# Layer 0's softmax sums from ones beside the values, moved into place by DMA

## The chip, the cores and the metric

The kernel runs on one core of one Trainium2 chip. The metric is device time in microseconds for one execution of the whole program. Several executions are timed and the median is given; one further execution is recorded by the hardware profiler, and all durations of single instructions come from that one.

## The reference

Four layers work on a batch of 16 sequences of 100 tokens with width 256 (`x`) and a context of 16 x 361 x 256 (`ctx_1024`). Only layer 0 matters for the change. It is a transformer decoder layer with 16 heads of 16 columns: masked self-attention, then cross-attention to the context, then a feed-forward layer, each followed by a layer norm.

```python
def _mha(xq, xk, xv, ..., causal):
    q, k, v = projections of xq, xk, xv              # (batch, 16 heads, tokens, 16)
    s = jnp.einsum('bhqe,bhke->bhqk', q, k) * (1.0 / math.sqrt(256))
    if causal: s = jnp.where(mask, s, -jnp.inf)
    w = jax.nn.softmax(s, axis=-1)                   # exp(s - max) / sum of exp
    o = jnp.einsum('bhqk,bhke->bhqe', w, v)
    return o (heads side by side) @ Wo.T + bo
```

The change concerns the division by the sum of the exponentials. Layer 1 (4 heads of 64), layer 2 (8 heads of 32 and a recurrent scan) and layer 3 follow and are not changed in what they do.

## The kernel before, in words

Activations are kept transposed, with the width on 128 partitions in two chunks (`c`), and in four groups (`g`) of four batches each, 400 columns a group. Products that need full precision are split into a high and a low part and made as three matmuls (`mm3`, L293). The order of the work on TensorE (PE), VectorE (DVE), ScalarE (ACT) and GpSimd (POOL) is the order in which the Python code issues it. Only the order of the DMA queue on SyncE (SP) is set by a scheduler, by its own estimate of times. Work that may run between the steps of a phase is written as generators and kept in a `Flow`: `flow.fill()` lets every generator in its side list take one step (the lists of weights, and `recips`) and then lets others run until one of them has issued matmuls. A generator that yields `REST` lets a step pass.

**Self-attention of layer 0** (`self_phase` with `nh` = 16) loops over 16 batches with two units each. A unit makes scores for eight heads in two PSUM banks (L1135, onto a mask, L854), takes maxima on DVE (L866), exponentials on ACT (L268), transposes on PE (L886) and copies those to SBUF on ACT (L595). When both units of a batch are done, `weigh` multiplies the transposed exponentials with the values (L588). The values of a batch lie in a tile `va` in which each head has 32 columns (`wide`): an even head has its 16 values in the first 16 of them, an odd head in the last 16, and the other 16 columns are zero. So the results of an even and an odd head, added in PSUM, land on the two halves of the same 32 partitions. The same pairs are formed once more with `cnt16` in place of the values (L903), 16 columns of ones and 16 of zeros: this gives each head's sum on the very partitions where its output is. ACT copies sums (L910) and outputs (L912), DVE takes the reciprocal (L913), POOL multiplies (L914), and `split_o` writes the high and low parts of the product to `oP` (POOL, L560 and L561). After every fourth batch the output projection follows (`epi_s0`).

Beside this phase, `split_context` brings the context in (L760), splits it on POOL (cast L763, difference L764) and stores both parts to DRAM (L496), one batch's part a step. Loads of it come back at L769, weights at L354.

**Cross-attention of layer 0** (`cross_phase` with `nh` = 16) loops over 16 batches with four units of four heads. The plan `"S01AV2Bb3CDmam"` gives the order within a unit: S scores (L824), digits maxima (L643), A to D the exponentials (L268, which also accumulate the sum of each row), a and b transposes (L665) with copies (L595 on ACT, L597 on DVE), V the weighing of the unit before the last (L588), m an attempt to finish a batch, followed by `flow.fill()`. DVE adds the odd heads' unit to the even heads' (L682, L684). The row sums of a batch's 16 heads go through `recips`: a reciprocal on DVE (L543), an expansion to 256 columns on ACT (L546), two transposes on PE (L553) and a copy on ACT (L555); POOL multiplies (L700). After the loop, `tail` issues what is left of the last two units among the first steps of the feed-forward phase.

Of the kernel before, what the change touches and what calls it, by code (L numbers as in the profile page):

```python
# [13 lines left out]
ALU = mybir.AluOpType  # L14
# [33 lines left out]
def tile_chain(ctx: ExitStack, tc: tile.TileContext, a: dict, out: bass.AP):  # L48
# [67 lines left out]
    nc.vector.tensor_reduce(parity[:, 0:1], sel4, AX.X, ALU.add)  # L116
    nc.vector.tensor_scalar(parity[:, 1:2], parity[:, 0:1], -1.0, 1.0, ALU.mult, ALU.add)

    cnt = const.tile([S, 112], F32, name="cnt")
    nc.gpsimd.memset(cnt, 1.0)  # L120
    nc.gpsimd.memset(cnt[:, 16:32], 0.0)
    cnt16 = [cnt[:, 0:32], cnt[:, 16:48]]
    cnt64 = cnt[:, 48:112]

    pexp = [const.tile([S, 4 * S], F32, name=f"P{i}") for i in range(6)]

    vals = []
    for i in range(2):
        t = const.tile([TC, NTC, 512], F32, name=f"va{i}")
        nc.gpsimd.memset(t, 0.0)  # L130
        vals.append(t)
    vals4 = [t[:, :, i * D : (i + 1) * D] for t in vals for i in range(2)]
    turns = {}
# [403 lines left out]
    def recips(ps, sums, nh, rests):  # L537
# [17 lines left out]
        nc.scalar.copy(rT, tp[:, : 2 * S])  # L555
        return rT

    def split_o(of, oP, bl):
        sl = slice(bl * S, (bl + 1) * S)
        nc.gpsimd.tensor_copy(oP[:, 0, :, sl], of)  # L560
        nc.gpsimd.tensor_tensor(oP[:, 1, :, sl], of, oP[:, 0, :, sl], ALU.subtract)  # L561
# [37 lines left out]
    def cross_phase(ps, nh, pro, load_kv, score, epi, plan, after=None, started=False, beat=None, late=None, **sets):  # L599

        units = head_units(nh)
        nu = nh // 4
        seq = [(b, u) for b in range(NB) for u in range(nu)]
        N = len(seq)
        kv, q, of, pts, pTs, total, scs, nms = {}, {}, {}, {}, {}, {}, {}, {}  # L610
        done, ended = [-1], []

        def kv_of(b):

            flow.front(
                ("kv", b), load_kv(b, lambda: nh != 16 or done[0] >= b - 2 and all(o[0] != "t" for o, _ in flow.q))
            )

        if not started:
            flow.put(("q", 0), pro(0))  # L620
            kv_of(0)

        def scores(n):
            b, u = seq[n]
            g, bl = b // GB, b % GB
            if u == 0:
                if bl == 0:
                    q[g] = flow.need(("q", g))
                    q[g, "o"] = pair(name="oP")
                    if g + 1 < NG:  # L630
                        flow.put(("q", g + 1), pro(g + 1))
                    elif after is not None:
                        after()
                kv[b] = flow.need(("kv", b))
                if b + 1 < NB:
                    kv_of(b + 1)
                total[b] = small.tile([S, 16], F32, tag="sums", name="sums")
            scs[n] = [ps.tile([P, 512], F32, tag="sc", name="sc") for _ in range(4)]
            score(q[g], bl, kv[b][0], units[u], scs[n])

        def high(n, i):
            nms[n, i] = nm = small.tile([S, 1], F32, tag="nm1", name="nm1", bufs=6)
            nc.vector.tensor_reduce(nm, scs[n][i][:S, :T], AX.X, ALU.max, negate=True)  # L643

        def soft(n, i):
            b, u = seq[n]
            h = units[u][i]
            pts[n, i] = pt = turn("P", pexp)
            look_up(
                pt[:, :T], scs[n][i][:S, :T], AF.Exp, **sets, bias=nms.pop((n, i)), accum_out=total[b][:, h : h + 1]  # L650
            )
            if i == 3:
                scs.pop(n)
                if u == nu - 1:
                    flow.put(("r", b), recips(ps, total.pop(b), nh, plan[plan.index("D") :].count("m")))

        def turned(n, *heads, tag="tp"):

            tps = []
            for i, _ in heads:  # L660
                pt = pts.pop((n, i))
                tp = ps.tile([P, 512], F32, tag=tag, name="pT_ps")
                made[0] += 1
                for c in range(NTC):
                    nc.tensor.transpose(tp[:TC, c * S : (c + 1) * S], pt[:, c * TC : (c + 1) * TC], ident[:S, :S])  # L665
                tps.append(tp)
            for (i, act), tp in zip(heads, tps):
                pTs[n, i] = pT = att.tile([P, 4 * S], F32, tag="pT", name="pT", bufs=NPT)
                evac(pT[:TC, : NTC * S], tp[:TC, : NTC * S], act)

        def weigh(n):
            b, u = seq[n]
            g, bl = b // GB, b % GB
            if u == 0:
                of[b] = att.tile([P, 2, S], F32, tag="of", name="of")
            o = ps.tile([P, 512], F32, tag="o", name="o_ps")
            made[0] += 1
            values(o, units[u], nh, kv[b][1], TC, lambda k, i: pTs[n, i][:TC, k * S : (k + 1) * S], NTC, nh > 4)
            if nh == 4:
                nc.vector.tensor_copy(of[b], o[:, : 2 * S].rearrange("p (c s) -> p c s", c=2))  # L680
            elif nh == 16 and u % 2:
                nc.vector.tensor_tensor(of[b][:, u // 2], o[:, :S], of[b][:, u // 2], ALU.add)  # L682
            else:
                nc.vector.tensor_copy(of[b][:, u // 2 if nh == 16 else u], o[:, :S])  # L684
            for i in range(4):
                pTs.pop((n, i))
            if u == nu - 1:
                kv.pop(b)
                done[0] = b
                ended.append(b)  # L690

        def finish():

            if not ended:
                return
            b = ended.pop()
            g, bl = b // GB, b % GB
            rT = flow.need(("r", b))
            f = of.pop(b)
            nc.gpsimd.tensor_tensor(f, f, rT.rearrange("p (c s) -> p c s", c=2), ALU.mult)  # L700
            split_o(f, q[g, "o"], bl)
            if bl == GB - 1:
                flow.put(("e", g), epi(g, q[g, "o"]))

        for n in range(N):
            for what in plan:
                if what == "S":
                    scores(n)
                    if n == 0 and flow.tailed():

                        flow.fill(2)
                    if n == 0:
                        clear_pads()
                elif what in "0123":
                    high(n, "0123".index(what))
                elif what in "ABCD":
                    soft(n, "ABCD".index(what))
                elif what == "a":
                    turned(n, (0, False), (1, True))
                elif what in "pq":  # L720
                    turned(n, ("pq".index(what), what == "q"))
                elif what == "V" and n >= 2:
                    weigh(n - 2)
                elif what == "V" and n == 0:
                    flow.end("t")
                elif what == "b" and n >= 1:
                    turned(n - 1, (2, False), (3, nh != 16))
                elif what in "rt" and n >= 1:
                    turned(n - 1, (2 + "rt".index(what), what == "t"))
                elif what == "m":  # L730
                    finish()
                    flow.fill()
                elif what == "s":
                    beat()

        def tail():

            weigh(N - 2)
            yield
            finish()  # L740
            turned(N - 1, (2, False), tag="mm")
            yield
            turned(N - 1, (3, True), tag="mm")
            yield
            weigh(N - 1)
            finish()
            yield

        if late is not None:
            late()  # L750
        flow.front(("t", None), tail())
# [76 lines left out]
    def self_phase(ps, nh, pro, w, score, epi, mask=None, beside=None, after=None, started=False):  # L828
# [61 lines left out]
                piece[b, h] = pT[:S, i * S : (i + 1) * S]  # L890

        def weigh(b):
            g, bl = b // GB, b % GB
            o = ps.tile([P, 512], F32, tag="o", name="o_ps")
            units = head_units(nh)
            half = len(units) // 2 or 1
            for us in (units[:half], units[half:]):
                for hs in us:
                    values(o, hs, nh, va[b], S, lambda k, i: piece[b, hs[i]], 1)
                for hs in us:  # L900
                    for h in hs:
                        c, r, cols, new, end = place(h, nh)
                        nc.tensor.matmul(  # L903
                            o[r, (2 + c) * S : (3 + c) * S], lhsT=cnt16[h % 2] if nh == 16 else cnt64,
                            rhs=piece.pop((b, h)), start=new, stop=end,
                        )
            va.pop(b)
            made[0] += 1
# [2 lines left out]
            of = att.tile([P, 2, S], F32, tag="of", name="of")  # L911
            nc.scalar.copy(of, o[:, : 2 * S].rearrange("p (c s) -> p c s", c=2))  # L912
            nc.vector.reciprocal(r, r)  # L913
            nc.gpsimd.tensor_tensor(of, of, r, ALU.mult)  # L914
            split_o(of, q[g, "o"], bl)
            if bl == GB - 1:
                flow.put(("e", g), epi(g, q[g, "o"]))

        def self_v(b):
            X, bl = q[b // GB][0], b % GB  # L920
# [787 lines left out]
```

## Time and profile before

| what | us |
|---|---|
| three timed executions | 1618.21, 1619.55 and 1625.3; median 1619.55 |
| the profiled execution, its own time | 1609.87 |
| its span from first to last instruction | 1608.2 |
| self-attention of layer 0, about | 25 to 205 |
| cross-attention of layer 0, about | 200 to 530 |
| granted TensorE clock, mean over the span | 0.959 of full |
| count matmuls with 32 columns (L903), whole span | 512 records, 21.7 busy |
| transposes of the expanded reciprocals (L553), all layers | 96 records, 16.8 busy |
| transfers issued on SP, whole span | 175 |

How to read it: the profile of one execution lists busy time of each engine, groups of equal instructions (count, busy time, mean length of one, idle time of the engine in front of them and what ended it), and the chain of waits: followed back from the last instruction, at each step to what released it. "PEld" is the weight load of TensorE and overlaps its matmuls. An fp32 matmul can appear as two records. "Granted clock" is the share of TensorE's full clock that the chip allowed in a stretch. SP has no busy time; its rows are the issues of transfers.

### The profile page before, as it was taken

The page shows a single profiled execution, that of the slowest core. Times are in us where ns is not written, and L with a number is a line of the kernel's source. Part 1 is how long each engine was busy: PE and PEld are TensorE (multiplying, and loading weights), DVE is VectorE, ACT ScalarE, POOL GpSimd, SP SyncE. Part 2 cuts the span into 40 slices and gives each one's busy share as a digit, 9 for nine tenths or more (in the row PEclk, how much of TensorE's full clock was granted, in tenths as well). Part 3 has the DMA queues.
Part 4 walks back from the last instruction along what each step waited for, and adds up shares of the span by engine and source line. Part 5 has one row for each costly group of instructions (what it writes and reads, how often), then busy time and mean ns, then how long its engine had stood idle before and what let it go on. Part 6 is the DMA issues. An engine that isn't in the chain of part 4 may idle for free.

```text
span 1608.2 us, 34891 instructions
## 1 busy us (share of the span) xinstructions
PE 1496.7 (93%) x13528; PEld 1320.5 (82%) x13528; DVE 924.6 (57%) x2137; ACT 811.4 (50%) x2301; POOL 692.6 (43%) x1136
## 2 busy tenths in 40 slices
PE   8999989999999989889999999998999999989998
PEld 6777777877777878779998889997888888878987
DVE  4565667777777663655534345556555555655553
ACT  4656756766766344641135553215455555555333
POOL 3435635565332445842257663133144444553300
PEclk9897999999998998999999999999999999998999
DMA  3343331121111000100013330010011111112085
GB/s 113 109 129 113 118 99 46 52 59 52 39 40 38 20 27 14 35 14 14 14 42 99 95 116 23 25 40 20 20 39 45 51 39 39 52 39 85 1 230 174
DMA packets 76501, 97.30 MB, mean 61 GB/s; under 512 B 3840, under 2 KB 76336, under 8 KB 76336
## 3 DMA queue, kind: packets, MB, share of 16 engines
q1 hardware_dynamic: 76336, 95.07, 19.7%
q8 instruction: 107, 1.75, 0.4%
q14 instruction: 58, 0.48, 0.1%
HBM read 81.49 MB, written 13.57 MB: 59 GB/s over the span
## 4 chain that ended last, share of the span: by engine, by line
PE 61%; DVE 11%; POOL 8%; ACT 8%; issue 8%; DMA 2%; SPq 0%; ACTq 0%; POOLq 0%; DVEq 0%
PE up_ps L293 12%; PE pT_ps L665 7%; PE down_ps L293 7%; PE lin_ps L293 5%; PE v_ps L293 5%; PE o_ps L588 5%; PE k_ps L293 4%; PE sc L824 4%; PE h_ps L1442 4%; ACT P L268 3%; DVE nm L643 2%; DMA cx<-cx 2%; PE pT_ps L886 2%; ACT L263 1%; PE sc L1135 1%
## 5 line engine op out<-in xcount | busy, mean ns | idle before, releaser
L268 ACT ACTIVATE P<-sc,nm 100x361 f32<-100x361 f32 (+1 forms) x678 | 314.2, 497 | 184.3 <-DVE nm L643 144.2
L643 DVE TENSOR_REDUCE nm<-sc 100x1 f32<-100x361 f32 x448 | 222.8, 525 | 100.5 <-PE sc L824 98.2
L665 PE MATMUL pT_ps<-ident,P 100*121 100x100 f32 x1344 | 212.8, 287 | 25.7 <-DVE pT L597 12.4
L293 PE MATMUL up_ps<-xp,w 128*128 128x400 f32 x1152 | 234.6, 354 | 2.2 <-DVE xp L300 1.1
L665 PEld LDWEIGHTS pT_ps<-ident,P 100*121 100x121 f32 x1344 | 176.4, 190 | 62.7 <-ACT P L268 20.8
L293 PEld LDWEIGHTS up_ps<-xp,w 128*128 128x128 f32 x1152 | 213.9, 192 | 7.9 <-DVE xp L300 2.0
L304 POOL TENSOR_TENSOR hp<-hid,hp 128x400 fp32r<-128x400 f32 x64 | 69.9, 1093 | 232.5 <-DVE hp L300 206.1
L293 PE MATMUL down_ps<-hp,w 128*128 128x400 f32 x768 | 155.8, 350 | 4.9 <-DVE x L988 1.8
L293 PEld LDWEIGHTS down_ps<-hp,w 128*128 128x128 f32 x768 | 141.3, 190 | 9.3 <-POOL hp L304 3.6
L597 DVE COPY pT<-pT_ps 121x300 f32<-121x300 f32 x287 | 127.1, 460 | 31.8 <-PE pT_ps L665 30.5
L588 PE MATMUL o_ps<-pT,va 121*32 121x100 f32 (+3 forms) x3328 | 127.6, 262 | 14.7 <-ACT f L322 2.8
L595 ACT COPY pT<-pT_ps 121x300 f32<-121x300 f32 (+2 forms) x273 | 110.9, 421 | 59.4 <-PE pT_ps L886 38.6
L588 PEld LDWEIGHTS o_ps<-pT,va 121*32 121x32 f32 (+3 forms) x3328 | 90.1, 118 | 56.6 <-issue 15.1
L293 PE MATMUL v_ps<-w,cx 128*121 128x256 f32 x864 | 131.5, 294 | 0.1
L293 PE MATMUL k_ps<-cx,w 128*128 128x362 f32 x576 | 116.8, 342 | 5.9 <-DMA cx<-cx 4.0
L293 PE MATMUL lin_ps<-xp,w 128*128 128x400 f32 x480 | 112.6, 375 | 8.0 <-DVE xp L300 5.2
L293 PEld LDWEIGHTS v_ps<-w,cx 128*121 128x121 f32 x864 | 110.6, 185 | 2.0 <-DVE of L682 0.5
L268 ACT ACTIVATE hid<-up_ps 128x400 f32<-128x400 f32 x64 | 32.4, 506 | 157.6 <-PE up_ps L293 148.9
L1442 PE MATMUL h_ps<-ht,raw 128*128 128x96 f32 (+4 forms) x792 | 107.8, 279 | 3.3 <-POOL ht L1456 1.6
L1442 PEld LDWEIGHTS h_ps<-ht,raw 128*128 128x128 f32 x792 | 98.1, 193 | 8.3 <-POOL ht L1456 7.1
L293 PEld LDWEIGHTS lin_ps<-xp,w 128*128 128x128 f32 x480 | 90.5, 203 | 14.3 <-DVE xp L300 4.9
L293 PEld LDWEIGHTS k_ps<-cx,w 128*128 128x128 f32 x576 | 94.6, 191 | 7.8 <-issue 4.4
(198 smaller groups left out, 2599.6 us busy)
## 6 DMA issues: line engine op xcount, KB each, us to landing
cx<-cx SPq DMA_DIRECT2D x80, 728.0 KB, 5.7
raw<-in_ctxT SPq DMA_DIRECT2D x16, 364.0 KB, 5.3
ct<-in_ctxp SPq DMA_DIRECT2D x16, 363.0 KB
raw<-in_L_Wf SPq DMA_DIRECT2D x8, 256.0 KB, 2.8
x<-in_xT SPq DMA_DIRECT2D x4, 400.0 KB
out<-y SPq DMA_DIRECT2D x8, 200.0 KB
raw<-in_L_ff_W1T SPq DMA_DIRECT2D x4, 256.0 KB
raw<-in_L_ff_W2T SPq DMA_DIRECT2D x4, 256.0 KB, 2.6
```

Source lines behind the costliest of these rows:

```text
L263: load = nc.scalar.preload_act_table_set(SETS[table["set"]][0]).ins
L268: table["used"].append(nc.scalar.activation(out_, in_, func, **kw).ins)
L293: nc.tensor.matmul(dst, lhsT=l, rhs=r, start=first and i == 0, stop=last and i == n - 1)
L304: nc.gpsimd.tensor_tensor(lo, src, hi, ALU.subtract)
L588: nc.tensor.matmul(o[r, at : at + S], lhsT=va[:rows, k, cols], rhs=pT(k, i), start=(new or alone) and k == 0, stop=(end or alone) and k == ...
L595: nc.scalar.copy(dst, src)
L597: nc.vector.tensor_copy(dst, src)
L643: nc.vector.tensor_reduce(nm, scs[n][i][:S, :T], AX.X, ALU.max, negate=True)
L665: nc.tensor.transpose(tp[:TC, c * S : (c + 1) * S], pt[:, c * TC : (c + 1) * TC], ident[:S, :S])
L824: nc.tensor.matmul(sc[:S, :TE], lhsT=lhs, rhs=k[r, lk, c, :TE], start=n == 0, stop=n == 2)
L886: nc.tensor.transpose(tp[:S, i * S : (i + 1) * S], pt[:, i * S : (i + 1) * S], ident[:S, :S])
L1442: nc.tensor.matmul(v[:, c], lhsT=wgh[:, k, c * P : (c + 1) * P], rhs=ht[:, k, :, t - n : t], start=k == 0, stop=k == 1,)
```

## The change

`va` is filled with ones instead of zeros (the values of each batch overwrite only their own 16 of 32 columns). A matmul with 32 columns of `va` then gives a head's output on 16 partitions and the head's sum on the 16 beside them. Even and odd heads are no longer added in PSUM but kept apart: `s4` has room for both (`[P, 2, 2, S]`, the first 2 for even and odd). `unmix` moves the 16-partition pieces with DMAs on SP: for each of even and odd and each of four 32-partition blocks, one transfer brings the sums onto the partitions of the outputs (`r`) and one brings the outputs (`of`). That is 16 transfers of 16 partitions x 200 elements a batch, for 16 batches of self-attention and 16 of cross-attention. `inverse` takes 1/r on ACT as Exp(-Ln r), after three (self) or four (cross) steps of its generator. In cross-attention the exponentials no longer accumulate sums, `recips` is not used for `nh` = 16, `finish` passes by as long as the inverse is not issued, and `tail` forces it. The sums and the count matmuls of self-attention (L903) are gone for `nh` = 16; layer 1 keeps them.

```diff
-    cnt = const.tile([S, 112], F32, name="cnt")
-    nc.gpsimd.memset(cnt, 1.0)
-    nc.gpsimd.memset(cnt[:, 16:32], 0.0)
-    cnt16 = [cnt[:, 0:32], cnt[:, 16:48]]
-    cnt64 = cnt[:, 48:112]
+    cnt64 = const.tile([S, 64], F32, name="cnt64")
+    nc.gpsimd.memset(cnt64, 1.0)
...
         t = const.tile([TC, NTC, 512], F32, name=f"va{i}")
-        nc.gpsimd.memset(t, 0.0)
+        nc.gpsimd.memset(t, 1.0)
...
+    def unmix(s4):
+        of = att.tile([P, 2, S], F32, tag="of", name="of")
+        r = att.tile([P, 2, S], F32, tag="rT", name="rT")
+        for i in range(2):
+            for j in range(P // 32):
+                own, other = (slice(32 * j + 16 * k, 32 * j + 16 * k + 16) for k in (i, 1 - i))
+                nc.sync.dma_start(r[own], s4[other, i])
+                nc.sync.dma_start(of[own], s4[own, i])
+        return of, r
+
+    def inverse(r, rests):
+        for _ in range(rests):
+            yield REST
+        look_up(r, r, AF.Ln)
+        look_up(r, r, AF.Exp, scale=-1.0)
+        return r
...
@@ cross_phase, soft @@
-            look_up(
-                pt[:, :T], scs[n][i][:S, :T], AF.Exp, **sets, bias=nms.pop((n, i)), accum_out=total[b][:, h : h + 1]
-            )
+            kw = {} if nh == 16 else {"accum_out": total[b][:, h : h + 1]}
+            look_up(pt[:, :T], scs[n][i][:S, :T], AF.Exp, **sets, bias=nms.pop((n, i)), **kw)
             if i == 3:
                 scs.pop(n)
-                if u == nu - 1:
+                if u == nu - 1 and nh != 16:
                     flow.put(("r", b), recips(ps, total.pop(b), nh, plan[plan.index("D") :].count("m")))
...
@@ cross_phase, weigh @@
-            if u == 0:
+            if u == 0 and nh == 16:
+                of[b] = twos[0].tile([P, 2, 2, S], F32, tag="s4", name="s4")
+            elif u == 0:
                 of[b] = att.tile([P, 2, S], F32, tag="of", name="of")
...
-            elif nh == 16 and u % 2:
-                nc.vector.tensor_tensor(of[b][:, u // 2], o[:, :S], of[b][:, u // 2], ALU.add)
             else:
-                nc.vector.tensor_copy(of[b][:, u // 2 if nh == 16 else u], o[:, :S])
+                nc.vector.tensor_copy(of[b][:, u % 2, u // 2] if nh == 16 else of[b][:, u], o[:, :S])
...
+                if nh == 16:
+                    of[b], r = unmix(of[b])
+                    flow.put(("r", b), inverse(r, 4))
 
-        def finish():
+        def finish(now=False):
 
-            if not ended:
+            if not ended or nh == 16 and not now and ("r", ended[-1]) not in flow.got:
                 return
...
@@ cross_phase, tail @@
+            finish(True)
             weigh(N - 2)
             yield
-            finish()
+            finish(True)
...
             weigh(N - 1)
-            finish()
+            if nh == 16:
+                yield REST
+                yield REST
+            finish(True)
             yield
...
@@ self_phase, weigh @@
+            if nh == 16:
+                made[0] += 1
+                for u, hs in enumerate(units):
+                    at = (u % 2 * 2 + u // 2) * S
+                    values(o[:, at : at + S], hs, nh, va[b], S, lambda k, i: piece.pop((b, hs[i])), 1, True)
+                va.pop(b)
+                s4 = twos[0].tile([P, 2, 2, S], F32, tag="s4", name="s4")
+                nc.scalar.copy(s4, o[:, : 4 * S].rearrange("p (i c s) -> p i c s", i=2, c=2))
+                of, r = unmix(s4)
+                flow.put(("w", ("out", b)), ending(b, of, r))
+                return
...
+        def outputs(b, of, r):
+            g, bl = b // GB, b % GB
             nc.gpsimd.tensor_tensor(of, of, r, ALU.mult)
             split_o(of, q[g, "o"], bl)
             if bl == GB - 1:
                 flow.put(("e", g), epi(g, q[g, "o"]))
+
+        def ending(b, of, r):
+            r = yield from inverse(r, 3)
+            outputs(b, of, r)
```

Lines in `@@` name the function that a piece is in.

## The prediction

> **What bounds the kernel now.** I read four views: the page, then busy time by stretch, then groups of instructions and the order of time in layer 0. From the page:
>
> ```profile
> PE 1496.7 (93%) x13528; PEld 1320.5 (82%) x13528; DVE 924.6 (57%) x2137; ACT 811.4 (50%) x2301; POOL 692.6 (43%) x1136
> PE 61%; DVE 11%; POOL 8%; ACT 8%; issue 8%; DMA 2%; SPq 0%; ACTq 0%; POOLq 0%; DVEq 0%
> ```
>
> TensorE is busy 93% of the span and holds 61% of the chain that ended last. Is that so where the change works? Busy time in two stretches, self-attention and cross-attention of layer 0 (columns: stretch, its length, then busy us and count of PE, PEld, DVE, ACT, POOL, then granted clock, DMA share, GB/s):
>
> ```profile
> 25.00:183.00 158.00, 146.90 (x1794) 118.13 (x1794) 93.03 (x166) 95.28 (x294) 67.65 (x80) 0.87 0.35 108
> 205.00:530.00 325.00, 300.76 (x3654) 245.41 (x3655) 234.22 (x590) 218.21 (x686) 145.76 (x180) 0.95 0.17 50
> ```
>
> PE is busy 93% of both, every other engine under 75%. So work taken off PE counts nearly in full, and the other engines matter where PE waits for them. Idle PE is 11 us in the first and 24 us in the second: a ceiling on what shorter waits can give.
>
> **Self-attention, removed.** The end of a batch's weighing, in order of time (start, length):
>
> ```profile
> 102.09 0.53 PE L903 MATMUL o_ps<-pT,cnt 100*32 100x100 f32 x16
> 102.43 0.53 PE L588 MATMUL o_ps<-pT,va 100*32 100x100 f32 x16
> 102.77 0.53 PE L903 MATMUL o_ps<-pT,cnt 100*32 100x100 f32 x16
> 103.42 0.33 ACT L910 COPY rT<-o_ps 128x200 f32<-128x200 f32 x1 [0.84 <-PE o_ps L903]
> 103.78 1.40 DVE L913 RECIPROCAL rT<-rT 128x200 f32<-128x200 f32 x1 [1.32 <-ACT rT L910]
> ```
>
> Blocks of 16 records start 0.34 us apart (102.09, 102.43, 102.77). The two counting blocks (L903) go, the value blocks stay: 2 x 0.34 x 16 batches = **-11 us**. The reciprocal leaves VectorE, 1.40 us and the wait in front of it (27.3 us in 13 times). VectorE has room; what PE gains lies between 0 and the 11 us that it idles. PE's named waits there are mostly for other work, so I take **-1**.
>
> **Self-attention, added.** ScalarE loses two copies (0.344 + 0.356 us), gains one of 128x400 (nearest row: 100x400, 0.50) and Ln and Exp of 128x200 (between a copy, 0.36, and the 128x400 Ln, 0.59; I take 0.40 each): +0.6 a batch, 10 us in all, hidden, since ScalarE is busy 95 of 158 us. Ln and Exp are in the table set already loaded.
>
> **The transfers.** Each of 32 batches gets 16 transfers on SP, each 16 partitions of 800 bytes. No row shows one of this shape. Nearest rows:
>
> ```profile
> 102.06 0.37 SPq L496 DMA_DIRECT2D cx<-cx  x1
> 65.43 0.37 SPq L496 DMA_DIRECT2D cx<-cx  x1
> 65.85 0.50 SPq L354 DMA_DIRECT2D raw<-in_L_c_WkT  x1
> L1315 SPq DMA_DIRECT2D raw<-in_L_Wg x1: 557/557/557, 1029.4 to 1029.4; - x1
> L1316 SPq DMA_DIRECT2D raw<-in_L_Wgc x1: 584/584/584, 1030.0 to 1030.0; - x1
> raw<-in_L_ff_W2T SPq DMA_DIRECT2D x4, 256.0 KB, 2.6
> cx<-cx SPq DMA_DIRECT2D x80, 728.0 KB, 5.7
> ```
>
> A lone issue is 0.37 us, back to back they start 0.42 to 0.51 apart, and transfers of 64 partitions take 0.56 and 0.58. I take 0.46, in the middle of the back-to-back rows, with ends 0.37 and 0.58. Landing: 2.6 us (256 KB row); below it only smaller, above it 5.7 if a cx transfer is ahead. So a batch's sums arrive 16 x 0.46 + 2.6 = 10.0 us after the copy that they read. In the program each transfer also waits for the one eight places before it: right behind a cx store of 5.7 us the eighth is held 5.7 - 8 x 0.46 = 2.0 us.
>
> The Trainium skill, page "DMA: Bandwidth & Descriptors", section "Rules for kernel authors", speaks against this: many small transfers should be coalesced, and under 64 KB one pays mostly overhead. The same page ("Anatomy of one DMA", fitted for transfers issued from GpSimd) gives about 2.0 us fixed; with that landing the 10.0 would be an estimated 9.4.
>
> Is 10.0 us too long in self-attention? Its period is (191.73 - 38.2) / 14 = 11.0 us (first copy L910 to the fifteenth), so about 10.3 afterwards. In ScalarE's order of the changed program Ln stands one batch plus two pT copies, a va copy and two heads' Exps behind the copy: 10.3 + about 3 = 13 us. Slack 3 us. SP's own load: 16 x 0.46, plus 34 older transfers in 14 batches, 2.4 x 0.46 = 1.1, makes 8.5 of 10.3 us. Behind a late Ln on ScalarE stand PE's pT copies; behind POOL's product stand the casts and differences of cx (0.92 + 1.75 us), and behind those, on SP, the store of cx and the next batch's transfers. That ring (0.75 Ln and Exp, 1.6 POOL, 2.7 cx, 0.9 two issues, 10.0) is 16 us against two periods, 20.6.
>
> **Cross-attention.** Removed on PE: two transposes a batch (L553, 0.26 us each if apart; overlapped pairs take 0.34 to 0.36): 0.26 to 0.36 x 16, I take **-5**. On ScalarE:
>
> ```profile
> L268 ACT ACTIVATION_READ_ACCUMULATOR P<-sc,nm 100x1 f32 x254 | 49.8, 196 | 0.0
> L546 ACT COPY rx<-rs 100x256 f32<-100x256 f32 x16 | 6.6, 413 | 1.4 <-DVE rs L543 1.4
> L555 ACT COPY rT<-rT_ps 128x200 f32<-128x200 f32 x16 | 5.1, 316 | 0.0
> ```
>
> The accumulator reads go. They overlap their neighbours: Exps start 0.55 us apart with them (330.45, 331.00, 331.54), 0.48 without (98.72, 99.20; wider data), so each costs 0.07 or a little more. rx and rT (0.73) make room for Ln and Exp (0.8). PE waits 19.9 us for these Exps in 26 places (pT_ps, L665); 0 to -6, I take **-2**.
>
> The added wait: the copy that ends a batch corresponds to the first row below, and Ln now stands behind the last Exp two units later:
>
> ```profile
> 335.45 0.25 DVE L682 TENSOR_TENSOR of<-o_ps,of 128x100 f32<-128x100 f32 x1
> 337.43 0.56 ACT L268 ACTIVATE P<-sc,nm 100x361 f32<-100x361 f32 x1 [0.50 <-DVE nm L643]
> 343.00 0.74 PE L824 MATMUL sc<-kc,two 32*100 32x362 f32 x12
> ```
>
> Unit starts are 333.78, 338.51, 343.00; the fourth Exp comes 3.65 after a start, so Ln stands at 343.00 + 3.65 + 0.5 = 347.1, which is 11.4 us behind the copy's end (335.7). Needed: 10.0. **Slack 1.4 us**, thin. Weight loads that wait for POOL stand within some batches' transfers on SP, cutting batches in halves. For late Lns in both phases: 0 to +8, I take **+1.5**.
>
> **The two ends.** From 190.65 to 208.5 the chain of waits runs through POOL's last cx, two stores and two loads of cx and into k_ps. Eight transfers of batch 15 now stand before the last store, eight behind: 0 to 16 x 0.46 = 7.4; I take **+3**. At the end of cross-attention the last copy ends at 530.1, so its sums land at 540.1, while Ln stands behind the fourth Gelu (534.7), with two table loads (1.28 each) and 0.8 around it. ScalarE is held 5.4 + 3.4 = 8.8 us; PE can run ahead on four score banks, about 5 us: 0 to +8.8, I take **+3.5**.
>
> **Sum**: -11 - 1 - 5 - 2 + 1.5 + 3 + 3.5 = **-11 us**. Against the profiled execution, 1609.87 (span 1608.2 and 1.7 around it): 1598.9. The median shown is 1619.55, 9.7 above; the same difference gives **1608.6** (-0.7%). About 0.5%, 8 us, is what a measurement here can tell from no change.
>
> **Rivals.** (1) **Sums come late in cross-attention**, the slower one: ScalarE stands at Ln and PE behind its Exps. It decides from (11.4 - 2.6) / 16 = 0.55 us a transfer, and in self-attention from (10.3 - 1.1) / 16 = 0.575. At 0.65, 16 x 0.10 = 1.6 us late in cross and 1.2 in self, over 16 batches each: +26 and +19, so -11 + 45 = +34, 1653. For it: the 64-partition rows. Against it: all full-width rows. At 0.58 it is only 0.5 us late in cross, 0.1 in self: -11 + 8 + 1, about -2.
> (2) **Gain eaten**: issue near 0.58, or transfers behind 5.7 us of cx in many batches, or the ends at their upper bounds (+10): -11 + 9 to 12, 1619.
> (3) **PE waits shrink too**: -12 - 4 - 6 - 6 + 3 = -25, 1594.
> That the change does nothing of what it says I can exclude: value copies write 16 of each 32 columns, so the ones stay, and the counting matmuls and transposes are gone from PE's order.
>
> **Numbers.** Forecast 0.42 (0.35 beyond 0.5%, 0.07 within), rival 3 0.10, rival 2 0.18 within, rival 1 0.30 slower. So faster 0.45, same 0.25, slower 0.30. The range runs from rival 3 (1594) into rival 1, to 1645; the faster cases alone span 1594 to 1611.
>
> **What would show it.** The stretch of self-attention shorter by 8 to 12 us and cross-attention by 3 to 7, no L903 form with 32 columns, issues near 0.46 on SP, and few waits of ScalarE for DMA at Ln. Wrong if ScalarE's waits for rT add up to tens of us, if SP is occupied without a gap in self-attention, or if the ends cost over 10 us.

## The result and the profile after

The changed kernel takes **1661.2 us**, the median of four executions (1655.95 to 1668.0), against 1620.3 for the kernel before, also of four (1618.21 to 1625.3). The ratio is **1.0258, with a 95% interval of 1.023 to 1.0286**: 41 us slower, where 11 us faster was forecast.

The profiled execution of the changed kernel is the slowest of its four (1668.0 us, span 1666.3), that of before (1609.87) is faster than all four of its own. So the two traces lie 58 us apart, 17 more than the medians; verdicts below go by the timed runs, the traces tell where. Three executions of the kernels below, one each of e4, e5 and e14 (1655.6, 5937.0 and 1631.6 us), were slow and are left out of the ratios, though not of the medians.

The page of after, in the two places that were shown of before:

```profile
PE 1505.9 (90%) x12984; PEld 1325.9 (80%) x12984; DVE 914.1 (55%) x2105; ACT 806.5 (48%) x2063; POOL 692.6 (42%) x1135
PE 54%; DVE 12%; issue 8%; POOL 8%; ACT 8%; SPq 5%; DMA 4%; ACTq 0%; DVEq 0%; POOLq 0%
```

TensorE has 544 records fewer and yet 9 us more of busy time. A queue that had 0% of the chain, SPq, now has 5%, and DMA has 4% for 2%.

Busy time by stretch (columns as before). First self-attention, then 40 us behind it, then cross-attention, moved by 44 us against the stretch shown of before:

```profile
25.00:183.00 158.00, 134.10 (x1207) 106.23 (x1208) 78.72 (x142) 90.77 (x275) 59.92 (x67) 0.78 0.32 96
225.00:245.00 20.00, 3.49 (x38) 2.70 (x38) 1.77 (x5) 3.58 (x9) 9.10 (x18) 0.61 0.44 138
245.00:265.00 20.00, 10.48 (x78) 8.32 (x77) 4.23 (x11) 5.03 (x11) 6.08 (x10) 0.53 0.36 114
249.00:574.00 325.00, 296.82 (x3629) 242.16 (x3630) 231.38 (x571) 201.57 (x430) 143.41 (x177) 0.95 0.20 58
```

Cross-attention is as it was (300.8 us of PE before, clock 0.95). Self-attention is not: all engines do less in the same 158 us, and the granted clock is 0.78 for 0.87. Behind it TensorE all but stands, 3.5 us of work in 20.

What SP does (order of time; start, length of the issue):

```profile
102.48 0.53 SPq L493 DMA_DIRECT2D cx<-cx  x1
103.11 0.45 SPq L782 DMA_DIRECT2D raw<-in_ctxT  x1
103.65 0.99 SPq L351 DMA_DIRECT2D raw<-in_L_ca_v_W  x1
104.69 0.49 SPq L351 DMA_DIRECT2D raw<-in_L_c_WvT  x1
105.34 0.52 SPq L563 DMA_DIRECT2D rT<-s  x1
105.95 0.54 SPq L564 DMA_DIRECT2D of<-s  x1
...
113.24 0.59 SPq L564 DMA_DIRECT2D of<-s  x1
113.87 0.59 SPq L563 DMA_DIRECT2D rT<-s  x1
114.50 0.59 SPq L564 DMA_DIRECT2D of<-s  x1
115.14 0.59 SPq L563 DMA_DIRECT2D rT<-s  x1
115.77 0.59 SPq L564 DMA_DIRECT2D of<-s  x1
116.45 0.53 SPq L493 DMA_DIRECT2D cx<-cx  x1
```

There is no gap here, and from 30 to 230 us only four of more than 0.3 us, 5.7 us together: the prediction's own sign of being wrong, SP occupied without a gap in self-attention, came nearly as written. Within a row the transfers start 0.63 us apart (113.24, 113.87, 114.50), so sixteen take 16 x 0.63 = 10.1 us, and context and weights come on top, once in a batch, when the row lets them through. The batches keep that pace: from the first to the fifteenth copy of the accumulators it is (214.29 - 38.78) / 14 = 12.5 us a batch, for 11.0 before. Who pays is seen in the waits from 25 to 220 us (in total, times, longest):

```profile
POOL cx L785 <- DMA raw<-in_ctxT: 65.5, 10, 10.5
DVE nm L888 <- PE sc L1174: 49.6, 20, 9.6
```

GpSimd waits 65.5 us for context whose load stands in SP's queue. And at the transition, in TensorE's order (idle time in brackets):

```profile
225.19 0.37 PE L604 MATMUL o_ps<-pT,va 100*32 100x100 f32 x6 [0.24 <-ACT pT L611]
235.88 1.54 PE L604 MATMUL o_ps<-pT,va 100*32 100x100 f32 x26 [10.32 <-ACT pT L611]
244.08 1.13 PE L680 MATMUL pT_ps<-ident,P 100*121 100x100 f32 x4 [6.00 <-POOL P L271]
254.24 2.15 PE L290 MATMUL k_ps<-cx,w 128*128 128x362 f32 x6 [9.03 <-DMA cx<-cx]
```

The k_ps at 254.24 is the one that stood at 208.48 before: 45.7 us late, 22 of them already there when the last masked scores of self-attention are made (213.5 for 191.5). From here to the first matmul of the feed-forward layer it takes 313.1 us, before 314.6.

The other 24 us are in SP's order between those masked scores and the read that this k_ps needs. Before, two stores of context parts and the read:

```profile
192.41 0.36 SPq L496 DMA_DIRECT2D cx<-cx  x1
199.20 0.36 SPq L496 DMA_DIRECT2D cx<-cx  x1
203.56 0.36 SPq L769 DMA_DIRECT2D cx<-cx  x1
```

After, three stores, each behind a row of transfers (or half a row), and the read behind the last eight:

```profile
221.74 0.53 SPq L493 DMA_DIRECT2D cx<-cx  x1
234.13 0.52 SPq L493 DMA_DIRECT2D cx<-cx  x1
243.05 0.53 SPq L493 DMA_DIRECT2D cx<-cx  x1
249.39 1.08 SPq L791 DMA_DIRECT2D cx<-cx  x2
```

From the masked scores to the read that is 203.56 - 191.50 = 12.1 us before and 249.39 - 213.45 = 35.9 after.

### The profile page after: what moved, and what is told of

It is laid out like the page before. It is cut to its first block, busy times and chain, and to the rows that moved or that the text cites. A ratio compares the mean times of both kernels' runs of the same rounds, so it can differ in the third digit from the quotient of the medians.

```text
span 1666.3 us, 34237 instructions
## 1 busy us (share of the span) xinstructions
PE 1505.9 (90%) x12984; PEld 1325.9 (80%) x12984; DVE 914.1 (55%) x2105; ACT 806.5 (48%) x2063; POOL 692.6 (42%) x1135
## 4 chain that ended last, share of the span: by engine, by line
PE 54%; DVE 12%; issue 8%; POOL 8%; ACT 8%; SPq 5%; DMA 4%; ACTq 0%; DVEq 0%; POOLq 0%
PE up_ps L290 11%; PE down_ps L290 6%; PE pT_ps L680 5%; PE lin_ps L290 5%; PE k_ps L290 4%; PE o_ps L604 4%; PE sc L846 4%; PE v_ps L290 4%; PE h_ps L1481 3%; DVE nm L659 3%; SPq L563 2%; SPq L564 2%; DMA cx<-cx 2%; ACT P L265 2%; PE pT_ps L908 1%
## 5 line engine op out<-in xcount | busy, mean ns | idle before, releaser
L265 ACT ACTIVATE P<-sc,nm 100x361 f32<-100x361 f32 (+1 forms) x678 | 308.1, 496 | 201.7 <-DVE nm L659 141.4
L659 DVE TENSOR_REDUCE nm<-sc 100x1 f32<-100x361 f32 x448 | 223.0, 525 | 111.4 <-PE sc L846 109.1
L290 PE MATMUL k_ps<-cx,w 128*128 128x362 f32 x576 | 120.2, 349 | 9.3 <-DMA cx<-cx 9.0
## 6 DMA issues: line engine op xcount, KB each, us to landing
rT<-s SPq DMA_DIRECT2D x256, 12.5 KB, 1.8
of<-s SPq DMA_DIRECT2D x256, 12.5 KB, 1.8
```

The lines of the kernel that those rows point to most:

```text
L265: table["used"].append(nc.scalar.activation(out_, in_, func, **kw).ins)
L290: nc.tensor.matmul(dst, lhsT=l, rhs=r, start=first and i == 0, stop=last and i == n - 1)
```

## The experiments

Fourteen kernels ran, in four groups; each group shares its own runs of the kernel before. The letters of the theories are explained in the expectations; A is always the same: SP's queue is full, and what stands behind the transfers on it is late. B means late sums in cross-attention in the first four and VectorE's order from e8 on. Milestones from the traces, in us from the start of the span: (a) last masked scores of self-attention, (b) the k_ps named above, (c) first matmul of the feed-forward layer.

| kernel | ratio to before, 95% interval | a | b | c |
|---|---|---|---|---|
| before | | 191.5 | 208.5 | 523.1 |
| the change | 1.0258 [1.023, 1.0286] | 213.5 | 254.2 | 567.3 |
| e1 change in self-attention only | 1.0289 [1.0241, 1.0336] | 213.1 | 253.2 | 564.8 |
| e2 change in cross-attention only | 1.0001 [0.9971, 1.003] | 192.1 | 209.2 | 519.9 |
| e3 before + 16 idle transfers | 1.0263 [1.0208, 1.0319] | 206.6 | 251.5 | 565.7 |
| e4 sums by way of DRAM | 1.013 [1.0052, 1.0207] | 207.2 | 227.3 | 553.8 |
| e5 before + 8 idle transfers | 1.0 [0.9961, 1.0039] | 189.8 | 210.3 | 521.8 |
| e6 before + 16 wide idle transfers | 1.0236 [1.0173, 1.0299] | 208.5 | 253.7 | 567.3 |
| e7 self-attention without transfers | 0.9986 [0.9953, 1.0018] | 192.6 | 207.4 | 519.2 |
| e8 8 transfers, outputs picked on VectorE | 1.0124 [1.0068, 1.0181] | 204.4 | 223.0 | 548.0 |
| e9 no counting matmuls | 0.9979 [0.9945, 1.0014] | 193.2 | 208.8 | 520.6 |
| e10 loads on GpSimd's queue | 1.0139 [1.0098, 1.0181] | 195.2 | 217.1 | 527.1 |
| e11 e10 + 16 idle transfers | 1.0246 [1.0196, 1.0296] | 197.3 | 232.6 | 544.4 |
| e12 the change + loads on GpSimd's queue | 1.0226 [1.0177, 1.0276] | 202.2 | 225.8 | 537.0 |
| e13 counting matmuls twice | 0.9997 [0.9968, 1.0026] | 192.2 | 208.4 | 520.3 |
| e14 8 transfers, sums only | 0.9988 [0.9954, 1.0023] | 193.4 | 208.1 | 525.0 |

### Which phase, and which part: e1 to e4

e1 keeps `cross_phase` of before and e2 `self_phase` of before; self-attention gets value tiles of its own, filled with ones (e1) or zeros (e2).

```diff
-            v = va[b] = turn("va", vals)
+            v = va[b] = turn("vs", valss) if nh == 16 else turn("va", vals)
```

> Self-attention as changed (with tiles of its own filled with ones), cross-attention as before. Theory A (issue rate): a 16-partition transfer takes SP 0.63 us, so 16 of them and the older transfers hold SP 11.3 to 12.5 us a batch, more than the 10.3 us that the rest of a batch would need, and the context parts that wait on the same queue pile up at the end of the phase. Then nearly the whole loss is here: 35 to 50 us over before, the second k_ps of cross-attention some 40 us later. Theory B (late sums): the loss comes from ScalarE standing at Ln, mostly in cross-attention, where the slack was thin; then this kernel is 0 to 12 us faster than before.

> Cross-attention as changed, self-attention as before (zero-filled tiles of its own). Theory A: SP has 19 us a batch here and is not full, so from 6 us faster than before to 4 us slower (gain 2 to 7 in the phase, 3 to 5 lost at its end). Theory B: slower than before by 15 us or more, with tens of us of waits at Ln.

Measured: 1663.6 and 1616.6 us, with 1617.0 for before. The whole loss is in self-attention and the transition behind it; cross-attention as changed costs nothing that the times show (interval -5 to +5 us). The rival of the prediction that put the loss at Ln in cross-attention falls.

e3 adds only transfers to the kernel before, and nobody reads what they bring:

```diff
             nc.vector.reciprocal(r, r)
+            if nh == 16:
+                for j in range(16):
+                    rows = slice(16 * (j % 8), 16 * (j % 8) + 16)
+                    nc.sync.dma_start(idle[rows], r[rows])
```

> The kernel before, with 16 transfers of 16 partitions x 200 a batch added on SP in self-attention, from the reciprocals into a tile that nobody reads; nothing is removed. Theory A: as slow as the change or slower, 35 to 60 us over before, though nobody waits for what they bring, because context and weights stand behind them. Theory B: within 3 us of before. Theory C (the lower granted clock, 0.935 against 0.959, is the cause and comes from the new matmul pattern): within 5 us of before.

Measured: 1659.7 us, the loss of the change to within the intervals. No late sum, no longer ScalarE order and no new matmul pattern is in this kernel, only the transfers (ScalarE and VectorE wait 5.2 us in 3 times for them to let go of a buffer). Whether it is SP's time or the traffic, e5 and e11 ask. Waits for the context look like those of the change (190 to 255 us):

```profile
PE k_ps L294 <- DMA cx<-cx: 20.2, 1, 20.2
...
POOL cx L764 <- DMA raw<-in_ctxT: 15.1, 2, 10.7
```

e4 sends the two halves of `s4` through DRAM, so that three issues a batch replace sixteen, and picks the outputs' rows on VectorE:

```diff
-                nc.sync.dma_start(r[own], s4[other, i])
-                nc.sync.dma_start(of[own], s4[own, i])
+            nc.sync.dma_start(AP of x for the half i, s4[:, i])
+        nc.sync.dma_start(r, AP of x with even and odd exchanged)
+        nc.vector.tensor_scalar(of, s4[:, 0], parity[:, 0:1], None, ALU.mult)
+        nc.vector.scalar_tensor_tensor(of, s4[:, 1], parity[:, 1:2], of, ALU.mult, ALU.add)
```

> As changed, but the sums go through DRAM in three 128-partition transfers a batch (two stores, one load that picks the neighbouring 16 partitions), and the outputs are picked by two masked operations on VectorE. Issues on SP fall from 16 to 3 a batch. Theory A: 8 to 20 us faster than before (1600 to 1612 for a median of 1620), since the work taken off TensorE then counts. Theory C: still 20 us or more slower than before, since the matmuls are those of the change. Theory B expects it faster than the change too, since store and load take about 6 us against 12.

Measured: 1643.1 us, by the ratio 21 us above before (8 to 33) and so some 20 better than the change, where a gain was expected: A explains the loss of the change and not this one. Two things were wrong in my picture: that the gain on TensorE would appear once SP is free (e7, e9 and e13 ask that), and that two short VectorE operations cost nothing (e8 and e14).

### How many, and is it the count or SP's time: e5 and e6

```diff
-                for j in range(16):
+                for j in range(8):
```

> The kernel before, with eight idle transfers a batch in self-attention where the sixteen were: 16 partitions of 800 bytes each, from the reciprocals into a tile that nobody reads. Theory A (SP is full: 16 x 0.63 + 1.2 us of older issues a batch of 11.0 us): eight take 5.0 + 1.2 = 6.2 of 11.0 us, SP is never full, and the time is that of before to within 5 us. Theory D (every transfer disturbs, by traffic or by memory access, and SP's order is not the matter): half of the 42 us that sixteen cost, about +21.

Measured: 1618.6 us, ratio 1.0. Half of the transfers cost nothing, sixteen cost 42 us: a threshold, as a queue has it, and no price for each transfer. SP's order in e5 has its gaps back (8 in 4.94 us, 0.62 each):

```profile
104.81 4.94 SPq L918 DMA_DIRECT2D idle<-rT  x8
109.85 0.53 SPq L761 DMA_DIRECT2D raw<-in_ctxT  x1
110.48 0.41 SPq L355 DMA_DIRECT2D raw<-in_L_c_WoT  x1
110.98 0.42 SPq L497 DMA_DIRECT2D cx<-cx  x1
111.45 0.50 SPq L761 DMA_DIRECT2D raw<-in_ctxT  x1
119.42 4.94 SPq L918 DMA_DIRECT2D idle<-rT  x8
```

e6 has the sixteen of e3 with 128 partitions of 25 elements each:

```diff
-                    nc.sync.dma_start(idle[rows], r[rows])
+                    nc.sync.dma_start(flat(idle)[:, cols], flat(r)[:, cols])   # cols: 25 of 200
```

> The kernel before, with sixteen idle transfers a batch of the same bytes as in e3, but each 128 partitions of 100 bytes in place of 16 partitions of 800. Theory A: what counts is the time that SP needs to issue them. At the 0.37 to 0.45 us of the full-width rows it is 16 x 0.42 + 1.2 = 7.9 of 11.0 us, and the cost is 0 to 8 us; if the trace shows them 0.6 us apart, it is that of e3, about +42. Theory D (the number of transfers or of bytes disturbs): +42 whatever the distance of the issues.

Measured: 1655.0 us, and its issues are not shorter (16 in 11.18 us from 106.50, 0.70 each):

```profile
106.50 11.18 SPq L918 DMA_DIRECT2D idle<-rT  x16
117.77 0.54 SPq L497 DMA_DIRECT2D cx<-cx  x1
118.36 0.51 SPq L761 DMA_DIRECT2D raw<-in_ctxT  x1
```

So it is A's second branch, and having only 16 partitions isn't what made 0.63 out of 0.37; what did was not tried. Because the shape did not shorten the issue, this run doesn't by itself part A from D; e5 does.

### Is there a gain on TensorE: e7, e9, e13

e7 is e1 without the transfers:

```diff
-                s4 = twos[0].tile([P, 2, 2, S], F32, tag="s4", name="s4")
-                nc.scalar.copy(s4, o[:, : 4 * S] ...)
-                of, r = unmix(s4)
+                nc.scalar.copy(of, o[:, : 2 * S] ...)
+                nc.scalar.activation(r, o[:, 2 * S : 4 * S] ..., AF.Square, scale=1e-3)
```

> Self-attention as changed but without the sixteen transfers, cross-attention as before. Two ScalarE copies read the accumulators, the second with Square, and Ln takes 1 + its argument, so that it stays finite: the outputs are not moved to their rows, so the attention's result is left out. The difference from e1 is the transfers alone, the difference from before is the gain on TensorE. Theory A: the gain is there, -8 to -12 us against before (the prediction's -11 - 1), and 50 us below e1. Theory C (the counting matmuls never bounded self-attention; the gain was not there to take): within 3 us of before.

Measured: 1617.7 us beside 1616.6 for before. The transfers and the waits for them are the whole of e1's loss (46 us between the two medians, which are of two groups), and **no gain shows below it** (-7.6 to +2.9 us): without the counting matmuls, without the reciprocal and without transfers self-attention ends where it did (a: 192.6 for 191.5).

e9 takes only the counting matmuls out, e13 issues them twice:

```diff
+                        if nh == 16:                        # e9
+                            piece.pop((b, h))
+                            continue
...
-            nc.scalar.copy(r, o[:, 2 * S : 4 * S] ...)      # e9
+            nc.scalar.copy(r, oner if nh == 16 else o[:, 2 * S : 4 * S] ...)
...
-                for hs in us:                               # e13
+                for hs in us + us if nh == 16 else us:
```

> The kernel before without its counting matmuls in self-attention (L903, 32 of 64 an accumulator): the copy that read the sums reads a constant tile of ones, and the reciprocal and everything else stay, so the division by the sums is left out there. TensorE has 11 us less to do and no other engine has more. Theory C1 (the gain on TensorE is real, and in e7 ScalarE's Ln and Exp, 0.8 us a batch or 13 us, took it): -8 to -11 us. Theory C2 (TensorE doesn't set the end of self-attention: other chains do, or the lower granted clock that follows idle time gives it back): within 4 us of before.

> The kernel before with the counting matmuls of self-attention issued twice (the second pass starts the sums anew): 2 x 0.34 us a batch more on TensorE, 11 us at the full clock. Theory C2 (TensorE's load doesn't set the length of self-attention within this range; the chain through ScalarE and VectorE and the granted clock do): 0 to +5 us. Theory P (the prediction's: TensorE's work counts in full): +10 to +14 us. If +11 here stands beside -3 for taking them away, the kernel before sits at the corner of the two.

Measured: 0.9979 and 0.9997, both intervals hold 1. Of the theories C2 is left: 11 us of TensorE's work, off or on, don't show in the time. (A gain of up to 9 us in e9 is inside its interval; -11 isn't, and +10 for e13 isn't either.) Where do they go? The same 180 us, self-attention to the transition, of before, e9 and e13:

```profile
25.00:205.00 180.00, 166.24 (x2048) 133.54 (x2048) 105.58 (x186) 109.95 (x341) 84.45 (x105) 0.89 0.36 109
```
```profile
25.00:205.00 180.00, 164.96 (x1534) 129.91 (x1534) 104.89 (x183) 110.32 (x340) 84.31 (x104) 0.82 0.35 108
```
```profile
25.00:205.00 180.00, 164.82 (x2561) 134.13 (x2561) 106.67 (x187) 110.58 (x341) 83.87 (x104) 0.96 0.35 109
```

TensorE is busy 165 to 166 us in each, with 2048, 1534 and 2561 records. What moves is the granted clock: 0.89, 0.82, 0.96. The same transposes of self-attention take 275, 296 and 263 ns:

```profile
L886 PE MATMUL pT_ps<-ident,P 100*100 100x100 f32 x256 | 35.4, 275 | 1.8 <-ACT P L268 1.7
```
```profile
L888 PE MATMUL pT_ps<-ident,P 100*100 100x100 f32 x256 | 39.9, 296 | 3.7 <-ACT P L270 3.6
```
```profile
L886 PE MATMUL pT_ps<-ident,P 100*100 100x100 f32 x256 | 33.0, 263 | 2.9 <-ACT P L268 2.7
```

Busy time times clock is 148, 135 and 158 us: work at the full clock does change by 10 to 13 us, and in these three traces the clock takes it up. It doesn't have to be the clock: e7, with 1532 records, was busy for 157.2 of the 180 us at 0.86, which is 135 us again, and ended self-attention at the same time with TensorE idle for 8 us more than in e9. One trace each, and the whole executions of the three differ (1609.9, 1622.2 and 1608.5 us), so the sizes are rough; the equal times are not from the traces. C2 names two reasons, other chains or the clock, and these runs don't part them. What sets the length of self-attention stays open: in the chain of waits of before, from 25 to 205 us, no line holds more than 9.8%.

### Is it what stands behind on SP: e10 to e12

```diff
-        nc.sync.dma_start(raw, view ...)          # weights; the same for the context's loads and stores
+        nc.gpsimd.dma_start(raw, view ...)
```

> Control for e11: the kernel before, with its weight loads, context loads and context stores (34 in self-attention's 14 batches) issued from GpSimd's queue in place of SP's. GpSimd has room (68 of 158 us busy in that stretch); 2.4 issues a batch. Both theories: 0 to +15 us, for GpSimd's own time for an issue, which no row here shows.

> e3 (sixteen idle transfers a batch on SP) with the weight and context transfers issued from GpSimd's queue as in e10, so that nothing of layer 0 but the reads of cx stands behind the idle transfers. Theory A (the loss of 42 us is the queue: weights and context stand behind the transfers on SP): within 8 us of e10. Theory E (the loss is SP's issuing or the transfers' traffic itself): 30 us or more above e10.

> The change itself with the weight and context transfers on GpSimd's queue. Here SP's sums are awaited: 16 x 0.63 + 1.8 = 11.9 us from copy to landing against 13 us of slack at Ln, and 10.1 of 11.0 us of SP's time a batch. Theory A: the loss against e10 shrinks from 41 to 0 to 20 us, what is left being the outputs' later products on GpSimd and the low clock. Theory E: 35 us or more above e10.

Measured: 1637.6, 1652.8 and 1651.3 us. e10 is dearer than expected (+20; 4 us of it by milestone c, the rest in later layers, whose weights also moved). Against it, the sixteen idle transfers, which cost 42 us in e3, slow self-attention by 2 us (a: 197.3 for 195.2): with the loads off SP, a full SP holds nearly nobody there. The rest of the 15 between e11 and e10 comes at the transition (b: 232.6 for 217.1), where the reads of cx were left on SP:

```profile
190.00 37.81 SPq L918 DMA_DIRECT2D idle<-rT  x54
227.97 1.12 SPq L770 DMA_DIRECT2D cx<-cx  x2
```

From 190 us on, 54 transfers are issued without a gap, and the reads stand behind them all; k_ps waits 13.6 us for one. So e11's bound of 8 us, which overlooked those reads, is missed, and in a way that shows the queue. e12, the change, comes to 14 above e10 where it was 41 above before, inside A's 0 to 20. Both readings take it that what e10 itself costs simply adds to the rest.

### Why fewer transfers did not win: e8 and e14

```diff
                 nc.sync.dma_start(r[own], s4[other, i])
-                nc.sync.dma_start(of[own], s4[own, i])
+        nc.vector.tensor_scalar(of, s4[:, 0], parity[:, 0:1], None, ALU.mult)                        # e8
+        nc.vector.scalar_tensor_tensor(of, s4[:, 1], parity[:, 1:2], of, ALU.mult, ALU.add)          # e8
+        nc.scalar.copy(of, s4[:, 0])                                                                 # e14
```

> The change with eight transfers a batch in place of sixteen in both phases: only the sums are moved, and the outputs are picked in place by two VectorE operations with the parity masks. Theory A (SP): 8 x 0.63 + 1.2 = 6.2 of 11.0 us, SP is not full, the transition is as before; left are the gain on TensorE, -11 and -1.5 in cross-attention, and two VectorE operations of some 0.3 to 0.7 us a batch: -10 to +5 against before. Theory B (what costs in e4 is not the transfers but the outputs picked on VectorE and the later sums, which hold the rows' maxima): +20 or more, as in e4.

> e8 without its two VectorE operations: the sums are moved by eight transfers a batch in both phases and awaited, and the outputs are copied by one ScalarE operation from the first half of the accumulator, so the picking of the outputs' rows is left out. Theory B (e8's 20 us are the two VectorE operations, which wait for ScalarE's copy in VectorE's order, ahead of the rows' maxima): -5 to +6 us against before. Theory F (they are the awaited sums, the later products on GpSimd): +15 or more.

Measured: 1639.6 us (+20) and 1618.9 us (0.9988). Eight awaited transfers a batch cost nothing that shows (at most 4 us by the interval), as eight idle ones do, and F falls: with the two VectorE operations 20 us are lost, with a ScalarE copy in their place none. In e8's order on VectorE:

```profile
84.29 0.56 DVE L889 TENSOR_REDUCE nm<-sc 100x4 f32<-100x400 f32 x1
88.04 0.94 DVE L564 TENSOR_SCALAR of<-s,parity 128x200 f32<-128x200 f32 x1 [3.18 <-ACT s L925]
89.01 1.87 DVE L565 SCALAR_TENSOR_TENSOR of<-s,parity,of 128x200 f32<-128x200 f32 x1
90.80 0.74 DVE L311 SCALAR_TENSOR_TENSOR w<-fuse_ps,w 128x256 fp32r<-128x256 f32 x2
```

VectorE stands 3.2 us for ScalarE's copy and works 2.8 more, and the weights' fusion queued behind it comes late. (These are long ones: the medians in self-attention are 0.32 and 0.43 us.) From 25 to 210 us that wait comes to 26.1 us in 12 times. Between e8 and e14, 15 us are lost by milestone b and 8 more in cross-attention.

That this wait is the reason, as B has it, is not shown, and a row of the kernel before speaks against it (25 to 205 us):

```profile
L913 DVE RECIPROCAL rT<-rT 128x200 f32<-128x200 f32 x16 | 22.4, 1402 | 33.9 <-ACT rT L910 33.9
```

There the reciprocal stood in the same place, waited longer for ScalarE (33.9 us) and worked longer (1.40 us a batch), and taking it away in e7 gained nothing. Why the two operations cost 20 us beside late sums stays open. e4 has the same two operations and the same wait (26.3 us in 11 times); that they make its loss too is likely and was not tried by itself.

None of these kernels is faster than the kernel before by more than its interval, so there was no better version to build from them.

## Why the prediction was wrong, step by step

**"So work taken off PE counts nearly in full"** failed first. The -11 and -1 of self-attention measure -2.3 us in e7 (interval -7.6 to +2.9) and -3.4 in e9 (-8.9 to +2.3). PE was busy 93% at a granted clock of 0.87, and that didn't make it a bound: in e13 it did some 10 us more of work (158 for 148 at the full clock) in the same time, at 0.96. The clock stood in the row that I quoted, and I didn't use it. What bounds the phase instead these runs don't say.

**"The transfers. I take 0.46"** failed in size, and it decided. The pitch is 0.63, above my upper end of 0.58: all my rows were of other transfers, between DRAM and SBUF. Landing was 1.8 us for 2.6. Late sums, which I derived the danger from, are the smaller part even so: 16 x 0.63 + 1.8 = 11.9 us against 13 at Ln, and in the change ScalarE waits at Ln 9.3 us in 2 places of self-attention (22.1 us in 5 from 25 to 600), while e3 loses as much with no sum to wait for. What breaks is the other sum that I made, **"SP's own load ... 8.5 of 10.3 us"**: 16 x 0.63 = 10.1, and 2.4 older issues at 0.5 to 1.0 us in the row (0.37 alone), make 11.3 to 12.5 of 11.0 us. So SP sets the pace, and the batches come 12.5 us apart. I treated SP's occupancy as a bound on the sums alone, and not on the context and weights that share the queue.

**"The two ends: I take +3"** for the transition. It follows from the step before: I put one batch's transfers around the last store, and they do stand there, eight ahead of it and eight ahead of the read. But the rows of the batches before stand between the stores as well (221.74, 234.13, 243.05), and milestone b is 24 us later than a explains (45.7 - 22).

**Cross-attention** was forecast at -5 - 2 + 1.5 + 3.5 = -2 (the 1.5 is for both phases), and e2 measures 0 with an interval of -5 to +5. That agrees and tests none of the four terms: milestone c of e2 is 519.9, and e7, e9 and e13, which leave cross-attention alone, have 519.2 to 520.6.

**Rival 1** named the price a transfer (0.65, 1653 us) nearly as it came, and that its time lies near the measured 1661 is half luck. Its sum for self-attention, (10.3 - 1.1) / 16 = 0.575 and +19 us, is the sum of a full SP, and a is 22 us late; but it charges that to late sums. Its other +26 are for Ln in cross-attention, where nothing was lost, and the 24 us of the transition, which it doesn't have, took their place.

With the measured terms the sum closes to 5 us, which is inside the intervals: 0 for TensorE's gain, 46 for the transfers in self-attention and at the transition (e1 less e7), 0 for cross-attention, against 41 measured.

The rule of the Trainium skill that I weighed, page "DMA: Bandwidth & Descriptors", section "Rules for kernel authors", which speaks for coalescing small transfers, pointed the right way. The same page says in "Issuing engines are not separate DMA queues" that the issuing sequencer's time is usually small beside the DMA; here the row of SP, 0.63 us of issue beside 1.8 us to landing, made it the bound. "Perfetto Trace Analysis", section "What 'DMA-bound' means", has this case: an issuing engine's track that is solid with DMA.

## What to carry to other kernels

Before adding transfers to a queue, add up its whole load a period, older transfers included, at the pitch of the new ones, and list what else stands on it in order: nobody has to wait for the new transfers for them to cost time. When TensorE looks full, look at its granted clock before pricing work at its busy time: here, at 0.89, 11 us more or less of work left the time as it was. Price no short operation by its length alone: two of 0.32 and 0.43 us cost 20 us in e8, for a reason that was not found.

## What the hardware showed that was not expected

- An issue on SP for a transfer from SBUF to SBUF took 0.59 us and 0.63 from start to start for 16 partitions of 800 bytes (the change, e3, e5), and 0.60 and 0.70 for 128 of 100 bytes (e6); a cx store in between took 0.53 instead of 0.37. On GpSimd's queue (e10) issues took 0.70 to 0.80:

```profile
103.60 0.78 POOL L496 DMA_DIRECT2D cx<-cx  x1 [0.30 <-POOL cx L764]
106.14 0.70 POOL L760 DMA_DIRECT2D raw<-in_ctxT  x1 [1.75 <-DVE w L314]
```

- In three traces with equal length and equal busy time the granted clock went with the amount of TensorE's work: 0.82, 0.89 and 0.96 for 1534, 2048 and 2561 records (e7, with less busy time, had 0.86 for 1532). The Trainium skill, page "TensorE: Matmul & The Clock Gate", section "Part 1: The HAM clock gate", has the clock at half after an idle window of about 3.4 us; in e9 the longest named wait of PE in these 180 us is 2.2 us, and the clock is at 0.82 all the same. Which short gaps the gate counts was not settled here.
